# One-hots for 32 node pairs per VectorE operation in the count-matrix build, and a finer turn for the convolution beside it

## The chip, the cores and the metric

The program runs on one core of one Trainium2 chip. A core has a matrix engine (TensorE, PE in the profile, with its weight loads listed apart as PEld), a vector engine (VectorE, DVE), a scalar engine (ScalarE, ACT), GpSimd (POOL), a queue engine (SyncE, SP) and 16 DMA engines that they share. [...]The metric is the device time of one execution in microseconds (us). Before the change it is 3608.37 us, the median of three runs from 3608.08 to 3612.73.

## The reference, cut to what matters

Four graph layers follow one another on a graph of N = 6250 nodes, 64 features each, with 206250 directed edges given as `src` and `dst`, sorted by `dst`. Each layer is `x = x + f(relu(layernorm(x)))`. Three of the four `f` are sums over neighbours with degree weights; the first, where the change lies, is

```python
norm = dinv[s] * dinv[d]
msgs = norm[:, None] * x[s]
agg = segment_sum(msgs, d, num_segments=n)
return agg @ W.T + b          # twice: 64 -> 128, relu, 128 -> 64
```

The third layer runs a small network over every edge and sums its messages per node, and the fourth repeats the neighbour sum three times.

## The kernel before, in words

The nodes are padded to 49 blocks of 128 (NP = 6272). The kernel doesn't gather along the edges: it builds the dense matrix of edge counts once, as 8-bit floats, and every neighbour sum is then a product with it. Everything here lies in the function `fast`.

**The stages.** First each edge becomes a pair of numbers (destination with the high part of the source; the low part of the source), written to DRAM. GpSimd's indirect DMAs fetch, for each of GC = 25 chunks of 128 node pairs, the edges of the chunk: `near2` (L872) finds the exact start, and `run` (L881) fetches 128 edges for each pair. VectorE and ScalarE turn a run into two digits (L885, L887), TensorE transposes them (L890), and VectorE copies them into the table `key` (L891). The comparisons `less` (L900) with the products of L904 count the degrees. When the last chunk is in, `deg` and `by_col` (L913 to L920) go through DRAM (L921, L924) and give `deg_dst` (L927), the norms (L682 to L688), and the scaled features split into three bf16 parts, `U3` (L934, and `split`, L711 to L715).

**The build.** The matrix is made in CS = 14 strips of CW = 448 destination columns, 224 node pairs. `build(s, q)` makes GB = 16 pairs: VectorE compares `key` with a count and writes two one-hot tensors, `hd` (128 x 1568, bf16) and `lo` (128 x 2048, bf16), both by L852; then, for each of two PSUM tiles of SG = 8 pairs, TensorE does eight products `lo` x `hd` into `p_a` (L861), one for each pair, and ScalarE copies the tile into the strip as 8-bit floats (L865). NQ = 14 builds make a strip. `lo` and `hd` come from a pool with two buffers each, so the one-hots of a build can only be written once TensorE is done with those two builds earlier. The finished strip is written to DRAM on SP's queue (L997).

**The convolution beside it.** While strip s is built, strip s - 1 is multiplied with `U3`: 147 products (49 blocks x 3 parts, L748, with a few more for the loops, L949) accumulate in `p_sum`. `convolve` is a Python generator that gives its turn away after each fourteenth of the blocks; the loop over q calls one build and then one turn of the convolution. Strip 0 is built before the norms are known, inside the loop over chunks (from chunk 3 on, one build per chunk); in strip 1 the turns are held back until half of the strip and then doubled. Beside every second strip runs `hidden`, which turns two strips' sums into the next features: products L739, L731, L970 and L975 on TensorE, `z` (L962, L979) and the split (L713, L715) on VectorE, and copies on ScalarE.

**The order of the work.** In this stage no order is written out by hand: the framework's scheduler decides in which order each engine gets its instructions when the program is built. After it, the first neighbour product over the whole matrix (L1026) reads `piece` tiles from DRAM; its first load stands on SP's queue behind the write of the last strip. From there on TensorE's and VectorE's orders are written out by hand. The third layer starts near 1040 us and is paced by GpSimd's gathers (L1354); the fourth ends the kernel.

Of the kernel before, what the change touches and what calls it, by code (L numbers as in the profile page):

```python
# [8 lines left out]
F32 = mybir.dt.float32  # L9
# [7 lines left out]
P = 128  # L17
N = 6250
D = 64
NB = 49  # L20
# [567 lines left out]
SW = 128  # L588
NG = NP // 2
GC = -(-NG // P)  # L590
GB = 16
GQ = 2
CW = 448
CS = NP // CW
# [22 lines left out]
def fast(ctx, tc, bad, x, src, dst, edge_attr, W3, b3, W4, b4, w1, b1, w2, b2, Bw, Bb, Cw, Cb,  # L617
# [73 lines left out]
    def normed(h, X_c):  # L691

        m = stat.tile([P, CB], F32, name="m")
        nc.vector.tensor_reduce(m, X_c, axis=AX.X, op=OP.add)
        nc.vector.tensor_scalar_mul(m, m, 1.0 / D)
        nc.vector.tensor_sub(h, X_c, over_features(m))
        q = stat.tile([P, CB, D], F32, name="q")
        nc.vector.tensor_mul(q, h, h)
        v = stat.tile([P, CB], F32, name="v")
        nc.vector.tensor_reduce(v, q, axis=AX.X, op=OP.add)  # L700
        nc.scalar.activation(v, v, AF.Sqrt, bias=eps, scale=1.0 / D)
        nc.vector.reciprocal(v, v)
        nc.vector.scalar_tensor_tensor(h, h, 0.0, over_features(v), op0=OP.max, op1=OP.mult)

    def of_nodes(pool):

        return pool.tile([P, NB, 3, D], BF16, name="U3")
# [47 lines left out]
    early_pool = early.enter_context(tc.tile_pool(name="early_pool", bufs=1, reuse_waits="tile"))  # L755
    with ExitStack() as ph:

        ipool = ph.enter_context(tc.tile_pool(name="ipool", bufs=1, reuse_waits="tile"))
# [71 lines left out]
        with ExitStack() as ps:  # L830
            psum = ps.enter_context(tc.tile_pool(name="ps0", bufs=1, space=PSUM, reuse_waits="tile"))
            p = psum.tile([P, SG, P], F32, name="p_a", bufs=2)
            nc.tensor.transpose(p[:D, 0, :], W3_sb, ident)
            nc.vector.tensor_copy(W3T, p[:D, 0, :])
            p = psum.tile([P, SG, P], F32, name="p_a", bufs=2)
            nc.tensor.transpose(p[:, 0, :D], W4_sb, ident[:D, :D])
            nc.vector.tensor_copy(W4T, p[:, 0, :D])

            H0 = ipool.tile([P, NB, D], F32, name="H0")
            for c in range(NC):  # L840
                normed(H0[:, blocks(c), :], X[:, blocks(c), :])

            NQ = CW // 2 // GB
            strips = {0: spool.tile([P, NB, CW], COUNT, name="strip")}

            def build(s, q):

                at = (s * CW // 2) + q * GB
                lo = opool.tile([P, GB // GQ, 128, GQ], BF16, name="lo")
                hd = opool.tile([P, GB // GQ, 2 * NB, GQ], BF16, name="hd")  # L850
                for t, of, k in ((hd, turns, 0), (lo, count, 1)):
                    nc.vector.tensor_tensor(  # L852
                        t, of.unsqueeze(1).to_broadcast(t.shape),
                        key[:, k, at:at + GB].rearrange("p (h j) -> p h j", j=GQ)
                        .unsqueeze(2).to_broadcast(t.shape),
                        op=OP.is_equal)
                for r in range(GB // SG):
                    p = psum.tile([P, SG, P], F32, name="p_a", bufs=2)
                    for j in range(SG):
                        g = r * SG + j  # L860
                        nc.tensor.matmul(p[:, j, :2 * NB], lo[:, g // GQ, :, g % GQ],  # L861
                                         hd[:, g // GQ, :, g % GQ], start=True, stop=True)
                    col = 2 * (q * GB + r * SG)

                    nc.scalar.activation(  # L865
                        strips[s][:, :, col:col + 2 * SG].rearrange("p b (j l) -> p b j l", l=2),
                        p[:, :, :2 * NB].rearrange("p j (b l) -> p b j l", l=2), AF.Copy,
                        saturate=False)

            for c in range(GC):  # L870
                near2 = rpool.tile([P, LOOK, 2], F32, name="near2")
# [7 lines left out]
            for c in range(GC):  # L879
                run = rpool.tile([P, P, 2], F32, name="run")  # L880
                nc.gpsimd.indirect_dma_start(  # L881
                    out=run.rearrange("p e t -> p (e t)"), out_offset=None, in_=pairs[:, :],
                    in_offset=bass.IndirectOffsetOnAxis(ap=exact_i[:, c:c + 1], axis=0))
                digits = rpool.tile([P, 2, P], BF16, name="digits")
                nc.vector.tensor_scalar(digits[:, 0, :], run[:, :, 0], start_of[:, c:c + 1], None,  # L885
                                        op0=OP.subtract)
                nc.scalar.activation(digits[:, 1, :], run[:, :, 1], AF.Copy)  # L887
                p = psum.tile([P, 1024], BF16, name="p_dig")
                for k in range(2):
                    nc.tensor.transpose(p[:, k * P:(k + 1) * P], digits[:, k, :], ident_b)  # L890
                nc.vector.tensor_copy(key[:, :, c * P:(c + 1) * P],  # L891
                                      p[:, :2 * P].rearrange("p (k s) -> p k s", k=2))
                if 0 <= c - 3 < NQ:
                    build(0, c - 3)
                if c % 9 == 8 or c == GC - 1:
                    c0 = c // 9 * 9
                    p = psum.tile([P, 512], F32, name="p_node")
                    for k in range(3):
                        less = rpool.tile([P, 9 * P], BF16, name="less", bufs=2)
                        nc.vector.tensor_scalar(  # L900
                            less[:, :(c + 1 - c0) * P], key[:, 0, c0 * P:(c + 1) * P],
                            float(k * NB), None, op0=OP.is_lt)
                        for i in range(c0, c + 1):
                            nc.tensor.matmul(p[:, k * 9 + i - c0:k * 9 + i - c0 + 1],  # L904
                                             less[:, (i - c0) * P:(i - c0 + 1) * P],
                                             count[:, 1, 0:1], start=True, stop=True)
                    nc.vector.tensor_copy(
                        below[:, :, c0:c + 1],
                        p[:, :27].rearrange("p (k i) -> p k i", k=3)[:, :, :c + 1 - c0])
# [7 lines left out]
            p = psum.tile([P, 512], F32, name="p_node")  # L917
# [7 lines left out]
            p = psum.tile([P, 512], F32, name="p_node")  # L925
# [6 lines left out]
            for c in range(NC):  # L932
                u = wpool.tile([P, CB, D], F32, name="z", bufs=2)
                nc.vector.tensor_mul(u, H0[:, blocks(c), :], over_features(norm0[:, blocks(c)]))  # L934
                split(u, U3, c)
# [4 lines left out]
            def convolve(s, strip):  # L940

                p = psum.tile([P, 512], F32, name="p_sum", bufs=2)
                for q in range(NQ):
                    for b in range(q * NB // NQ, (q + 1) * NB // NQ):
                        if b == NB - 1:
                            for d in range(s * CW // P, -(-(s + 1) * CW // P)):
                                lo_, hi_ = max(d * P, s * CW), min((d + 1) * P, (s + 1) * CW)
                                for k in range(3):
                                    nc.tensor.matmul(  # L949
                                        p[k % 2 * D:(k % 2 + 1) * D, lo_ - s * CW:hi_ - s * CW],  # L950
                                        U3[:, d, k, :], ident_b[:, lo_ - d * P:hi_ - d * P],
                                        start=False, stop=False)
                        spread(p, U3, b, strip[:, b, :], CW)
                    yield
                if s % 2 == 0:
                    y[s // 2] = (wpool if s < CS - 2 else early_pool).tile([P, W], F32, name="y")
                nc.scalar.activation(y[s // 2][:, s % 2 * CW:(s % 2 + 1) * CW], p[:, :CW], AF.Copy)
# [25 lines left out]
            for s in range(CS):  # L983
                if s:
                    strips[s] = spool.tile([P, NB, CW], COUNT, name="strip")
                strip = strips[s]
                for q in range(NQ):
                    if s:
                        build(s, q)
                    if s == 1 and q < NQ // 2:  # L990
                        continue
                    for steps in beside * (2 if s == 1 else 1):
                        next(steps, None)
                for steps in beside:
                    for _ in steps:
                        pass
                nc.sync.dma_start(strip_of(s, slice(0, NB)), strip)  # L997
                beside = [convolve(s, strip)]
                if s and s % 2 == 0:
                    beside.append(hidden(s // 2 - 1, wpool, psum))  # L1000
# [496 lines left out]
    with ExitStack() as ph:  # L1497
# [5 lines left out]
        for layer in range(3):  # L1503
# [25 lines left out]
            else:  # L1529
                for s in range(CS):  # L1530
# [3 lines left out]
                    t = whole[:, :, s % 2 * CW:(s % 2 + 1) * CW]  # L1534
                    p = psum.tile([P, 512], F32, name="p_sum", bufs=2)
# [48 lines left out]
```

## Time and profile before

| what | value |
|---|---|
| device time, median of three runs | 3608.37 us |
| device time of the profiled execution | 3611.97 us |
| span of the profiled execution | 3610.2 us |
| busy over the span: TensorE, weight loads, VectorE, ScalarE, GpSimd | 84%, 59%, 54%, 34%, 46% |
| busy from 210 to 558 us: TensorE, weight loads, VectorE, ScalarE | 346.80, 229.57, 323.02, 255.43 of 348 us |
| mean TensorE clock, 100 to 157 us and 210 to 558 us | 0.57 and 1.00 |
| L852 `hd`, `lo`: operations, mean | 196 and 196; 974 and 1222 ns |
| L861 products, L865 copies | 3136; 392 at 820 ns |
| first product of the first convolution | 156.89 us |
| last one-hots begin, last strip's write is issued | 555.68 us, 559.11 us |

The profile is of one execution. Busy shares are means over stages with different limits, so the table also gives the stretch in which the matrix is built beside the convolution. [...]where one group follows another without a gap, the start times say more than the busy share. An operation's duration is from its start to its end as recorded; on VectorE the next one can start before that end, and the start-to-start time is what an operation costs in a full queue. "Idle before" names what released an engine.

### The profile page before, as it was taken

The page shows a single profiled execution, that of the slowest core. Times are in us where ns is not written, and L with a number is a line of the kernel's source. Part 1 is how long each engine was busy: PE and PEld are TensorE (multiplying, and loading weights), DVE is VectorE, ACT ScalarE, POOL GpSimd, SP SyncE. Part 2 cuts the span into 40 slices and gives each one's busy share as a digit, 9 for nine tenths or more (in the row PEclk, how much of TensorE's full clock was granted, in tenths as well). Part 3 has the DMA queues.
Part 4 walks back from the last instruction along what each step waited for, and adds up shares of the span by engine and source line. Part 5 has one row for each costly group of instructions (what it writes and reads, how often), then busy time and mean ns, then how long its engine had stood idle before and what let it go on. Part 6 is the DMA issues. An engine that isn't in the chain of part 4 may idle for free.

```text
span 3610.2 us, 59581 instructions
## 1 busy us (share of the span) xinstructions
PE 3039.4 (84%) x24393; PEld 2141.2 (59%) x24393; DVE 1954.2 (54%) x3899; ACT 1239.3 (34%) x2024; POOL 1665.0 (46%) x1889
## 2 busy tenths in 40 slices
PE   1699999999977777878878887878887888799999
PEld 0466667999954444444444444444454444489998
DVE  6899993532235546556555655655655565531111
ACT  1577772000023434434333443434433444210000
POOL 4200001000037777777777777777777777400000
PEclk9699999999988888889889888888988888799999
DMA  3233335565532223223323232322332322256664
GB/s 107 64 91 95 95 95 189 188 205 183 178 101 80 77 53 84 71 70 97 86 68 97 70 85 79 88 68 76 91 88 70 94 70 68 81 166 194 196 206 143
DMA packets 229312, 388.76 MB, mean 108 GB/s; under 512 B 137573, under 2 KB 139743, under 8 KB 228771
## 3 DMA queue, kind: packets, MB, share of 16 engines
q1 hardware_dynamic: 170420, 321.51, 28.3%
q0 software_dynamic: 55104, 60.65, 8.3%
q8 instruction: 193, 3.16, 0.4%
q10 hardware_dynamic: 3504, 2.70, 0.3%
q14 instruction: 91, 0.75, 0.1%
HBM read 340.47 MB, written 44.24 MB: 107 GB/s over the span
## 4 chain that ended last, share of the span: by engine, by line
POOL 35%; PE 35%; issue 14%; DMA 9%; DVE 5%; ACT 1%; POOLq 0%; DVEq 0%; SPq 0%; ACTq 0%
POOL v L1354 35%; PE p_acc L1026 21%; PE p_sum L748 7%; DMA v<-Vp_dram,src_g 7%; PE p_a L861 4%; DMA near<-pairs,begin_i 1%; PE p_node L739 1%; DMA piece<-A 1%; DVE lo L852 0%; DMA run<-pairs,exact_i 0%; PE p_acc L1023 0%; PE p_node L970 0%; PE p_bc L1380 0%; DMA X<-in_x 0%; PE p_node L975 0%
## 5 line engine op out<-in xcount | busy, mean ns | idle before, releaser
L1354 POOL DMA_INDIRECT v<-Vp_dram,src_g x1616 | 1592.1, 985 | 859.9 <-issue 828.6
L1026 PE MATMUL p_acc<-U,piece 128*128 128x192 bf16 x9604 | 817.7, 246 | 5.0 <-DMA piece<-A 5.0
L1026 PEld LDWEIGHTS <-piece 128*128 128x128 fp8e4 x9604 | 798.9, 98 | 17.0 <-DMA piece<-A 5.2
L1380 PE MATMUL p_bc<-BC,h 128*128 128x256 f32 x1616 | 585.8, 496 | 0.0
L1389 DVE TENSOR_TENSOR m<-gate,v 128x512 f32<-128x512 f32 x202 | 140.3, 694 | 762.5 <-DMA v<-Vp_dram,src_g 627.7
L1380 PEld LDWEIGHTS p_bc<-BC,h 128*128 128x128 f32 x1616 | 341.2, 234 | 154.7 <-issue 116.2
L1396 ACT ACTIVATE m<-m 128x512 bf16<-128x512 f32 x202 | 127.2, 630 | 821.9 <-DVE m L1391 821.9
L748 PEld LDWEIGHTS <-U 128*64 128x64 bf16 x4116 | 231.1, 112 | 215.4 <-issue 68.3
L1036 DVE TENSOR_REDUCE zg<-p_acc 128x128 f32<-128x384 f32 x112 | 56.3, 507 | 537.4 <-PE p_acc L1026 536.9
L865 ACT ACTIVATE strip<-p_a 128x784 fp8e4<-128x784 f32 x392 | 302.3, 820 | 112.6 <-PE p_a L861 112.0
L1376 PE MATMUL p_bc<-BC_b,ones 3*128 3x512 bf16 x404 | 180.9, 448 | 167.3 <-DVE m L1390 167.2
L1260 PE MATMUL p_sum<-ident_b,piece 128*128 128x128 bf16 x1372 | 154.9, 238 | 183.7 <-DVE junk L1266 183.4
L1260 PEld LDWEIGHTS <-piece 128*128 128x128 fp8e4 x1372 | 117.7, 107 | 318.8 <-issue 301.2
L1376 PEld LDWEIGHTS <-ones 3*128 3x128 bf16 x404 | 37.5, 93 | 439.4 <-DVE m L1390 235.3
L1366 PE MATMUL p<-h,w_d 128*128 128x512 f32 x404 | 253.5, 713 | 38.6 <-ACT h L1370 38.6
L748 PE MATMUL p_sum<-piece,U 128*64 128x448 fp8e4 x2058 | 238.1, 374 | 27.0 <-DVE junk L1266 18.7
L1370 ACT ACTIVATE h<-p,b_c 128x512 f32<-128x512 f32 x404 | 255.8, 684 | 12.9 <-PE p L1366 12.6
L1266 DVE SCALAR_TENSOR_TENSOR junk<-p_sum,there 128x512 bf16<-128x512 f32 (+1 forms) x392 | 242.1, 618 | 27.3 <-PE p_sum L1260 18.7
L748 PE MATMUL p_sum<-strip,U 128*64 128x448 fp8e4 x2058 | 242.0, 359 | 2.5 <-ACT U L711 1.4
L852 DVE TENSOR_TENSOR lo<-count,key 128x2048 bf16<-128x2048 bf16 x196 | 239.6, 1222 | 0.0
L861 PEld LDWEIGHTS <-lo 128*128 128x128 bf16 x3136 | 164.7, 103 | 98.6 <-DVE lo L852 75.8
L861 PE MATMUL p_a<-hd,lo 128*128 128x98 bf16 x3136 | 195.1, 217 | 32.6 <-DVE lo L852 31.1
(198 smaller groups left out, 3308.5 us busy)
## 6 DMA issues: line engine op xcount, KB each, us to landing
piece<-A SPq DMA_DIRECT2D x249, 784.0 KB, 4.3
e<-in_edge_attr SPq DMA_DIRECT2D x202, 256.0 KB, 2.7
A<-strip SPq DMA_DIRECT2D x14, 2744.0 KB, 13.1
v<-Vp_dram,src_g POOLq DMA_INDIRECT x1616
there<-A SPq DMA_DIRECT2D x28, 784.0 KB
pairs<-pair SPq DMA_DIRECT2D x1, 1616.0 KB, 5.3
Vp_dram<-v SPq DMA_DIRECT2D x7, 224.0 KB
out<-X SPq DMA_DIRECT2D x6, 224.0 KB
```

What stands on the lines that cost most here:

```text
L748: nc.tensor.matmul(p[half * D:(half + 1) * D, :w], U3[:, b, k, :], at_block, start=(i < 2), stop=(i >= 3 * n - 2))
L852: nc.vector.tensor_tensor(t, of.unsqueeze(1).to_broadcast(t.shape), key[:, k, at:at + GB].rearrange("p (h j) -> p h j", j=GQ) .unsqueeze(2 ...
L861: nc.tensor.matmul(p[:, j, :2 * NB], lo[:, g // GQ, :, g % GQ], hd[:, g // GQ, :, g % GQ], start=True, stop=True)
L865: nc.scalar.activation(strips[s][:, :, col:col + 2 * SG].rearrange("p b (j l) -> p b j l", l=2), p[:, :, :2 * NB].rearrange("p j (b l) -> ...
L1026: nc.tensor.matmul(p[d // 2][:, d % 2 * 3 * D:(d % 2 + 1) * 3 * D], t[:, b, d * P:(d + 1) * P], U3[:, k * CB + b, :, :].rearrange("p t f - ...
L1260: nc.tensor.matmul(p[:, a - a0, :], held["here", i, k][:, a, b * P:(b + 1) * P], ident_b, start=True, stop=True)
L1266: nc.vector.scalar_tensor_tensor(junk[:, :(a1 - a0) * P], p[:, :a1 - a0, :].rearrange("p a q -> p (a q)"), 15.5, of_there, op0=OP.min, op1 ...
L1354: nc.gpsimd.indirect_dma_start(out=v[:, j, :], out_offset=None, in_=Vp_dram[:, :], in_offset=bass.IndirectOffsetOnAxis(ap=src_g[:, g, j:j ...
L1366: nc.tensor.matmul(of[g][p], w, of[g].pop(x), start=True, stop=True)
L1370: nc.scalar.activation(of[g][t], of[g].pop(p), **how)
L1376: nc.tensor.matmul(p_bc[:, 4 * b:4 * b + 4].rearrange("p j o f -> p (j o f)"), ones, BC_b, start=True, stop=False)
L1380: nc.tensor.matmul(p_bc[:, 2 * q:2 * q + 2].rearrange("p j o f -> p (j o f)"), h2[:, q * P:(q + 1) * P], BC, start=False, stop=(k == 1))
```

## The change

GB goes from 16 to 32. A build covers 32 node pairs: one `hd` of 128 x 3136 and one `lo` of 128 x 4096, then four PSUM tiles. NQ, the builds per strip, becomes 7. `build` becomes a generator that gives its turn away after every second PSUM tile, the loop takes 2 x NQ steps, and the convolution is cut into 2 x NQ turns, so that a turn still follows on every 16 pairs. Strip 0's builds come at chunks 3, 5, ... 15 instead of at every chunk from 3 to 16. The one-hots' four buffers take twice the space; to make room, `H0`, the normed features, lies in the memory of `V3` instead of in a tile of its own (`V3` is first written much later, by `hidden`).

```diff
-GB = 16
+GB = 32
@@
-            H0 = ipool.tile([P, NB, D], F32, name="H0")
+            H0 = of_nodes(early_pool).rearrange("p b t f -> p (b t f)").bitcast(F32)[
+                :, :NB * D].rearrange("p (b f) -> p b f", f=D)
@@ build: at the end of the loop over PSUM tiles
+                    if r % 2:
+                        yield
@@ loop over chunks
-                if 0 <= c - 3 < NQ:
-                    build(0, c - 3)
+                if c >= 3 and c % 2 and (c - 3) // 2 < NQ:
+                    for _ in build(0, (c - 3) // 2):
+                        pass
@@ convolve
-                for q in range(NQ):
-                    for b in range(q * NB // NQ, (q + 1) * NB // NQ):
+                for q in range(2 * NQ):
+                    for b in range(q * NB // (2 * NQ), (q + 1) * NB // (2 * NQ)):
@@ loop over strips
-                for q in range(NQ):
+                for q in range(2 * NQ):
                     if s:
-                        build(s, q)
-                    if s == 1 and q < NQ // 2:
+                        if q % 2 == 0:
+                            built = build(s, q // 2)
+                        next(built, None)
+                    if s == 1 and q < NQ:
                         continue
                     for steps in beside * (2 if s == 1 else 1):
                         next(steps, None)
```

## The prediction

> **What bounds the kernel now.** I read the page first, to place the change: the build and the first convolution lie between 55 and 560 us, and the rest is another matter (from 1040 us GpSimd's gathers, then a full TensorE). Nothing after 560 us is touched by the diff, so the question is when that stage ends. I then took busy time by stretches. Columns: stretch, its length, then PE, PEld, DVE, ACT, POOL with counts, PE clock, DMA share, GB/s.
>
> ```profile
> 100.00:157.00 57.00, 33.20 (x370) 27.14 (x370) 47.60 (x88) 31.65 (x53) 12.18 (x12) 0.57 0.29 79
> 210.00:558.00 348.00, 346.80 (x4401) 229.57 (x4401) 323.02 (x330) 255.43 (x351) 0.00 (x0) 1.00 0.33 89
> ```
>
> Two regimes. From 210 us TensorE and VectorE both look full; before 157 us VectorE is the busiest and TensorE waits. [...]here the weight loads are at 66%; so I took start times from the chain that ended last (start, length, what), where the two are closest to a tie:
>
> ```profile
> 307.75 0.86 PE p_a L861 x16
> 308.62 1.26 PE p_sum L748 x12
> 309.87 0.86 PE p_a L861 x16
> 310.73 1.06 PE p_sum L748 x9
> 311.79 0.85 PE p_a L861 x16
> ```
>
> Each group starts when the one before ends. TensorE needs 0.855 + 1.06 and 0.855 + 1.26, so 4.03 us per 32 pairs, and leaves no gap. VectorE's timeline over the same time:
>
> ```profile
> 308.22 1.23 DVE L852 TENSOR_TENSOR lo<-count,key 128x2048 bf16<-128x2048 bf16 x1
> 309.36 0.98 DVE L852 TENSOR_TENSOR hd<-turns,key 128x1568 bf16<-128x1568 bf16 x1
> 310.24 1.23 DVE L852 TENSOR_TENSOR lo<-count,key 128x2048 bf16<-128x2048 bf16 x1
> ```
>
> Start to start: lo 1.135, hd 0.885, so 2.02 per 16 pairs and 4.04 per 32: a dead tie. What breaks it is `hidden`. Two strips repeat every 63.4 us (L739 starts at 209.65, 272.96, 336.34, 399.75). TensorE's share of that: 28 x 0.855 + 14 x (1.06 + 1.26) + hidden's 1.71 + 1.09 + 1.89 + 1.71 + L949's 0.7 = 63.5 us. VectorE's: 28 x 2.02 + 4 x 0.55 = 58.8. So TensorE is the bound, and VectorE waits for it; the waits of 209.65 to 526.49 us (who, for whom: total, times, longest) agree:
>
> ```profile
> PEld L861 <- DVE lo L852: 35.2, 95, 0.5
> DVE hd L852 <- PE p_a L861: 13.9, 15, 1.1
> ```
>
> The first line looks like the opposite, but its 0.37 us each is the weight queue's pause at a change of group, which also stands there with "issue" as the cause, while the matmuls of the chain run on without a gap.
>
> Before 157 us, the chain passes through VectorE and the loads of the edges:
>
> ```profile
> 119.78 0.70 ACT strip L865
> 120.50 0.83 ACT strip L865
> 121.45 6.60 DMA run<-pairs,exact_i
> 128.15 0.32 ACT digits L887
> 128.47 0.69 issue
> 129.17 5.60 DMA run<-pairs,exact_i
> 135.18 0.88 DVE hd L852
> ```
>
> Loads of `run` that took 2.67 us at 57.05 take 6 us here: strip 0's write went out at 121.34.
>
> [...]from durations, (1222 - 974)/(2048 - 1568) = 0.517 ns per element and 164 ns fixed; start to start, 0.521 ns and 68 ns. [...]lo takes 1222. [...]at 0.57, 16 products of L861 take 1.49 us, at 1.00 0.855.
>
> **The change part by part.**
>
> *One-hots.* 392 operations become 196. Estimated from the slope: hd 164 + 3136 x 0.517 = 1785 ns, lo 2282 ns; start to start 1.70 and 2.20, 3.90 us per 32 pairs against 4.04. VectorE gains 2 x 0.068 = 0.137 us per build of 32: 13.4 us over 98. From 167 us on, TensorE's own 63.5 us per two strips hide this: worth nothing there. Were TensorE not the cover it would be worth 0.96 us a strip.
>
> *TensorE's groups.* In the changed program as built, the steady order is the old one (16 products of p_a, then 9 or 12 of p_sum), with one group more per two strips (8 and 8 with 3 between). A change of group costs roughly 0.15 us (12 products of L748 take 1.26 in company, 12 x 0.0937 = 1.12 in the run of 147 at 558.75): 6 x 0.15 = +0.9. A few groups of p_a at 0.88 to 0.93 wait for lo, 0.17 us per two strips; gone: -1.0. Sum zero, ends -3 and +3.
>
> *Buffers.* Two of 32 pairs: hd of build n + 2 waits for all 32 products of n. VectorE has 3.90 for TensorE's 4.03; queued behind a waiting hd are lo and hidden's z, r and U. In the new queue z (L962) stands before a build that TensorE needs some 9.5 us after L739; z and that build take 0.6 + 3.9. At r and U, lo is done about 0.5 us ahead of need. Taken as zero; the end is a rival below.
>
> *H0's place.* V3's first write, near 224 us, is long after H0's last read (L934, near 165). The waits of `piece` loads and of GpSimd's DMAs are as before, but for two loads that lose a wait for VectorE. Nothing.
>
> *The start.* Here the order does change. VectorE's queue, up to by_col (L920), held 19 builds of 16; now 12.5 of 32, i.e. 25. Up to deg_dst 23 become 28, and before the first convolution starts TensorE has done 480 pairs' products instead of 384. Step by step, from 99.04 us (last `near` in):
>
> - VectorE then has 8 x 3.90 + 1.70 for builds 5 to 13's hd, plus 40 small operations, about 8.1: 41.0 us, by_col at 140.0 if never idle. Before, the same stretch was 33.5 of work and 10.4 idle (6.8 on late runs, the rest mostly on transposes queued behind p_a), by_col at 143.01. The larger builds sit in those gaps. Strip 0 is done some 5 us earlier, so its write meets runs 20 to 24 rather than 21 to 24, and three buffers of `run` hold the fetch back as before: I allow 3.5 idle, by_col 143.5. Ends: 140 (no idle), 147 (a lo of 2.2 us holds up the near gathers, a microsecond at each of four).
> - by_col to deg_dst took 8.4 (through DRAM, by two SP issues; VectorE has 6.1 of builds beside): 151.9.
> - deg_dst to the convolution's stream took 7.74 (to 159.16); hd, lo and hd between grow by 0.82 + 1.07 + 0.82: 10.4, so 162.3.
> - Then 168 products at 0.0937 and L949, 16.2, and 1.8 for the low clock at the start (before: 67 in 8.31): 180.3. The kernel before reached the same sum of work (480 pairs, 168 products) at 179.07 + 2 x 0.855 + 1.06 + 1.26 = 183.1.
>
> So 2.8 us less. The idle TensorE waits longer at the start, but has more of its work behind it. All that follows is TensorE-bound to the last p_a, then the fixed chain copy, strip write, first `piece` (559.72 + 19.2). Sum: -2.8 from the start, 0 in the steady part. The profiled execution took 3611.97 (span 3610.2) and would take 3609.2; the median 3608.4 becomes **3605.6 us**.
>
> **Rivals.**
>
> *A smooth start.* If the builds fill the idle time, by_col comes at 140 and the gain is 6: 3602. For it: 10 us of idle in VectorE's queue. Against: [...]a build stands where it stands.
>
> *A late start.* `near` and `run` wait behind operations of 2.2 us and three buffers: by_col 147 to 149, 3609 to 3611. For it: POOL's 1.25 us cadence leaves little slack. Against: POOL's own issues pace it until 97 us.
>
> *VectorE was the bound.* Then 0.137 x 7 x 13 = 12.5 us come off: 3596. For it: 94% busy. Against: the chain without gaps, and 13.9 us of waiting for TensorE.
>
> *Slower: two buffers starve TensorE at r and U.* Those wait for ScalarE's copies, which can stand behind two evictions (2 x 0.77 = 1.54 us); beyond the 0.5 us of slack that is 1.0 us each, 2.0 per two strips, 12 over six: 3605.6 + 12 = 3617. It decides once r or U comes more than 0.5 us late.
>
> **How the numbers follow.** Chances: forecast 0.58 (own range 3603 to 3608.5, from the ends of the sum), smooth start 0.15, late start 0.15, VectorE bound 0.05, starved 0.07. The measurement tells 0.2%, 7.2 us, from nothing. Faster by more: VectorE bound and a third of the smooth start, 0.10; slower: starved, 0.07; the rest, 0.83, is within. The range 3600 to 3611.5 takes in forecast, late start and most of the smooth one.
>
> **What would show it.** Right: L852's forms at about 1.78 and 2.28 us; PE without gaps from about 165 us and two strips every 63.4; the first convolution's product near 160, later than 156.89; the last strip's write about 3 us earlier than 559.11. Wrong: gaps of PE before L861 with VectorE as releaser, a two-strip period off by over 0.5 us, or by_col outside 140 to 147.

## The result and the profile after

The changed kernel takes 3618.78 us (median of 7 runs, 3615.66 to 3623.62) against 3610.11 for the kernel before (7 runs, 3606.16 to 3612.73): ratio 1.0031, 95% interval 1.0022 to 1.0040. It is slower by 8.7 us where 2.8 us less was forecast, and lies above the top of the range. The profiled execution took 3618.26 us (span 3616.5).

Busy time by stretches of the changed kernel (columns as before):

```profile
100.00:157.00 57.00, 30.99 (x361) 27.11 (x362) 46.07 (x70) 28.95 (x47) 22.34 (x16) 1.00 0.32 88
210.00:558.00 348.00, 347.25 (x4369) 229.35 (x4369) 312.72 (x176) 254.46 (x350) 0.00 (x0) 1.00 0.33 91
```

In the steady stretch VectorE's busy time fell by 10 us (323.02 to 312.72), and TensorE stayed full: worth nothing, as predicted. The number to look at is in the first line. GpSimd has 16 instructions where it had 12, and they take 22.34 us instead of 12.18. (The clock of 1.00 in that line, against 0.57 before, isn't a difference in speed: 16 products of L862 take 1.49 to 1.53 us there, as they mostly do in the kernel before, and 0.85 in the steady stretch. The trace of the changed kernel has no record of the clock before 177.7 us, and the view counts that as full.)

Milestones in the two traces, in us:

| | before | after | difference |
|---|---|---|---|
| last reduce of `near` ends | 99.12 | 107.51 | +8.4 |
| `by_col` starts | 143.01 | 157.15 | +14.1 |
| 480 pairs and 168 products of the convolution done | 183.17 | 192.09 | +8.9 |
| first `to_nodes` of the hidden chain (L739) | 209.65 | 218.58 | +8.9 |
| mean period of two strips after it | 63.37 | 63.82 | +0.45 |
| first `piece` load | 559.72 | 571.17 | +11.5 |

So there are two losses: about 9 us before 210 us, and 0.45 us in each later pair of strips. (The runs of the changed kernel alone differ by 8 us, 3615.66 to 3623.62, and in the undisturbed traces the part behind the first `piece` load takes 3045 to 3052 us, so one pair of traces doesn't give the 8.7 exactly.)

The smaller loss first. The chain that ended last, changed kernel, steady part:

```profile
235.75 1.06 PE p_sum L748 x9
236.81 0.48 PE p_a L862 x8
237.29 0.50 PE p_sum L748 x3
237.79 0.48 PE p_a L862 x8
238.27 1.06 PE p_sum L748 x9
```

This is the split group of the prediction, 8 and 8 products of `p_a` with 3 of `p_sum` between them. From 236.81 to 239.33 TensorE needs 2.52 us for 16 products of `p_a` and 12 of `p_sum`; unsplit they took 0.855 + 1.26 = 2.115. That is 0.40 us for two more changes of group, nearly the whole 0.45.

The larger loss shows on GpSimd. The timeline of the changed kernel, VectorE and then GpSimd (start, length):

```profile
71.41 1.78 DVE L853 TENSOR_TENSOR hd<-turns,key 128x3136 bf16<-128x3136 bf16 x1
73.86 2.29 DVE L853 TENSOR_TENSOR lo<-count,key 128x4096 bf16<-128x4096 bf16 x1
```

```profile
70.86 0.95 POOL L875 DMA_INDIRECT near<-pairs,begin_i  x1 [0.30 <-issue]
72.11 1.90 POOL L875 DMA_INDIRECT near<-pairs,begin_i  x1 [0.30 <-issue]
74.32 2.64 POOL L884 DMA_INDIRECT run<-pairs,exact_i  x1 [0.30 <-issue]
```

The gather at 72.11 starts inside `hd` (71.41 to 73.19) and ends 0.82 us after it, at 74.01. The one at 74.32 starts inside `lo` (73.86 to 76.15) and ends at 76.96, 0.81 us after it. The one at 70.86, which had run for 0.55 us when `hd` began, keeps its 0.95 us. None of them waits for a semaphore: the time is inside the instruction. The kernel before has the same, at half the length; again VectorE, then GpSimd:

```profile
66.89 1.22 DVE L852 TENSOR_TENSOR lo<-count,key 128x2048 bf16<-128x2048 bf16 x1
```

```profile
67.49 1.43 POOL L872 DMA_INDIRECT near<-pairs,begin_i  x1 [0.30 <-issue]
```

67.49 + 1.43 = 68.92, which is 0.81 us after `lo`'s end at 68.11. Up to the last gather of `near` GpSimd goes from one gather straight to the next in both kernels (0.30 us between them), so the whole stretch can be added up. Before: 37 gathers, 36 steps of 1.25 us, and 2.3 us of holding make 47.3 (47.46 from the first start to the last). After: 38 gathers (one more `run` stands ahead of the last `near`), 37 steps and 9.6 us of holding make 55.9 (56.05). The 8.6 us between them are 7.3 of holding and one step of 1.25. Holding is here the time by which the gathers exceed 0.95 us each.

### The profile page after: what moved, and what is told of

It is laid out like the page before. It is cut to its first block, busy times and chain, and to the rows that moved or that the text cites. A ratio compares the mean times of both kernels' runs of the same rounds, so it can differ in the third digit from the quotient of the medians.

```text
span 3616.5 us, 59295 instructions
## 1 busy us (share of the span) xinstructions
PE 3046.1 (84%) x24393; PEld 2148.2 (59%) x24393; DVE 1945.4 (54%) x3703; ACT 1240.5 (34%) x2024; POOL 1676.5 (46%) x1889
## 4 chain that ended last, share of the span: by engine, by line
PE 35%; POOL 34%; issue 14%; DMA 9%; DVE 6%; ACT 2%; POOLq 0%; DVEq 0%; SPq 0%; ACTq 0%
POOL v L1360 34%; PE p_acc L1032 20%; PE p_sum L748 7%; DMA v<-Vp_dram,src_g 7%; PE p_a L862 4%; PE p_node L739 1%; PE p_bc L1386 1%; DMA run<-pairs,exact_i 1%; DMA piece<-A 1%; DVE lo L853 0%; DMA near<-pairs,begin_i 0%; PE p_acc L1029 0%; PE p_node L974 0%; DVE hd L853 0%; DVE q L698 0%
## 5 line engine op out<-in xcount | busy, mean ns | idle before, releaser
L862 PE MATMUL p_a<-hd,lo 128*128 128x98 bf16 x3136 | 203.1, 220 | 33.9 <-DVE lo L853 24.2
L862 PEld LDWEIGHTS <-lo 128*128 128x128 bf16 x3136 | 170.6, 104 | 98.9 <-issue 67.0
L853 DVE TENSOR_TENSOR lo<-count,key 128x4096 bf16<-128x4096 bf16 x98 | 223.8, 2284 | 0.0
```

The costliest lines, as they stand in the source:

```text
L853: nc.vector.tensor_tensor(t, of.unsqueeze(1).to_broadcast(t.shape), key[:, k, at:at + GB].rearrange("p (h j) -> p h j", j=GQ) .unsqueeze(2 ...
```

## The experiments

Theory L: the loss is made at the start, where VectorE's operations of twice the length hold GpSimd's gathers. Against it stood S (the loss lies in the steady part or in the buffers of 32), O (what counts is the block of a build in VectorE's queue and the order around it) and H (H0's place). Later the start itself was parted into N (the hold of `near` makes the loss) and R (the longer queue and the held `run` gathers after `near` make it). In all diffs `pairs_of(s)` is the number of pairs in a build of strip s, and `w` the number in one VectorE operation.

One thing has to be known to read the numbers. The runs were made in sets, each beside the kernel before on the same chip. Three of the sets fell on chips on which the kernel before itself takes 4125 to 4160 us with a spread of over 1%, so that their ratios tell nothing under 0.3%. There TensorE and ScalarE also paused in the start, with operands ready: TensorE for 2 to 6 us at a time in the first of these sets, ScalarE for 11.5 and 5.9 us in e5_again. These chips are called disturbed below. Most of what ran on them was run again on chips where the kernel before takes 3609.6 to 3610.1 us; the table at the end of this section holds only those and the changed kernel's own result.

**Which strips lose: 16 first, then 32 (e1), and the reverse (e2).**

```diff
-    return 32
+    return 16 if s < 2 else 32      # e1; e2: 32 if s < 2 else 16
```

> Builds of 16 pairs for strips 0 and 1, of 32 for strips 2 to 13; the rest as in the changed kernel (H0's place, a turn after every second PSUM tile). Theory L (the loss is made at the start: VectorE's operations of 1.8 and 2.3 us hold up GpSimd's gathers of near and run): the start is that of the kernel before, last near reduce 99, by_col 143, 480 pairs and 168 products near 183; only the steady part's +0.45 us per two strips is left, so +2.5 us against the kernel before, ratio 1.0007. Rival S (the loss is in the steady part, or in two buffers of 32): as slow as the changed kernel, ratio 1.0025 to 1.003.

> The other half: builds of 32 pairs for strips 0 and 1, of 16 for strips 2 to 13. Theory L: last near reduce at 106 to 108, by_col at 154 to 158, the common point of 480 pairs and 168 products near 191 to 192, then a period of 63.4 us per two strips; +7 to +9 us, ratio 1.002 to 1.0025. Rival S: ratio 1.000.

On a chip of the disturbed kind e1 had its last `near` at 105.7, `by_col` at 149.8 and L739 at 216.3; e2 107.8, 157.9 and 218.6. Ratios 1.0001 (0.9973 to 1.0029) and 1.0007 (0.9987 to 1.0026). e2's start was the changed kernel's; e1's was not that of the kernel before. Both were run again:

> Builds of 16 pairs for strips 0 and 1, of 32 for strips 2 to 13, once more, since the first chip's times spread over 1% and its TensorE paused. Theory L (the loss is made at the start, by the length of VectorE's operations): on a chip without the pauses last near reduce at 99, by_col at 143, the steady part +2.5 us; ratio 1.0007. Rival S (steady part): 1.0025 to 1.003. Rival H (H0's place): last near reduce at 105, by_col at 149, ratio 1.002.

> Builds of 32 pairs for strips 0 and 1, of 16 for strips 2 to 13, once more. Theory L: last near reduce at 107 to 108, by_col at 157 to 158 as on the first chip, a period of 63.4 us per two strips, ratio 1.0015 to 1.0025. Rival S: 1.000.

e1: last `near` 100.1, `by_col` 143.9, L739 at 210.4, period 63.88, ratio 1.0005 (0.9996 to 1.0013). e2: 107.4, 156.8, 217.4, period 63.40, ratio 1.0020 (1.0013 to 1.0028). The two halves of the change carry the two losses: up to the first `piece` load e1 loses 2.7 us and e2 7.1 against the kernel before on the same chip, together 9.7; the changed kernel, on another chip, lies 10.6 above it. S falls.

**H0's place alone (e4).**

```diff
-            H0 = ipool.tile([P, NB, D], F32, name="H0")
+            H0 = of_nodes(early_pool).rearrange("p b t f -> p (b t f)").bitcast(F32)[
+                :, :NB * D].rearrange("p (b f) -> p b f", f=D)
```

> The kernel before with one edit of the change alone: H0 lies in the tile that later holds V3. Theory L and rivals S and O: nothing, ratio 0.9995 to 1.0005. Rival H (the shared place makes V3's first writes or the loads of the third layer wait): up to +3 us, ratio 1.001.

Ratio 0.9986 (0.9966 to 1.0007), but last `near` at 105.1 and `by_col` at 149.2, on the disturbed chip. H0's place or the chip? The kernel before was therefore run unchanged beside e1 to e3:

> The kernel before, instruction for instruction, as one more run beside the others on their chip. In the first set of runs TensorE paused for 2 to 6 us several times between 63 and 104 us, with its operands ready, in the kernels whose first strips have operations of 16 pairs, and last near reduce fell at 105. Theory C (that is the chip): on a chip that pauses, this kernel too has its last near reduce at 104 to 106 and by_col at 148 to 150; on one that doesn't, 99 and 143. Rival H (it is H0's place, which those kernels share and this one lacks): 99 and 143 on any chip.

It landed on an undisturbed chip: last `near` 99.6, `by_col` 143.6, L739 at 210.5, ratio 0.9999 (0.9991 to 1.0008). That doesn't tell what it would do on the other. What decides is e1_again on this same chip: it has H0's new place and starts within 0.5 us of it. H0's place costs nothing, and the 6 us of e4 go with the chip.

**Builds of 32 with two operations of 16 (e3).**

```diff
-                w = n
+                w = 16
```

> Builds of 32 pairs in buffers of 32, as in the changed kernel, but each one-hot is made by two VectorE operations of 16 pairs. Theory L (the length of one operation counts): no GpSimd gather takes over 1.45 us, the sums of 25 near and 25 run fall back to 25 to 26 us each, last near reduce at 99 to 101, by_col at 143 to 147; ratio 0.9995 to 1.001. Rival O (what counts is that a build of 32 stands in VectorE's queue as one block, at every second chunk, whatever its operations): last near reduce at 104 to 108, by_col over 150, ratio 1.002 to 1.003.

> Builds of 32 pairs, each one-hot made by two VectorE operations of 16 pairs, once more. Theory L: the sums of 25 near and 25 run fall to 25 to 27 us each; last near reduce at 99 to 101, by_col at 143 to 147, ratio 0.9995 to 1.001. Rival O (the block of a build in VectorE's queue counts, whatever its operations): by_col over 150, ratio 1.002 to 1.003.

First try, on the disturbed chip: last `near` 101.8, `by_col` 149.8, ratio 0.9997 (0.9971 to 1.0024). Second: 98.9, 145.3, L739 at 210.4, period 63.41, ratio 1.0002 (0.9994 to 1.0010). The gathers of the changed kernel and of e3 (busy us and mean ns, then the idle time before them):

```profile
L884 POOL DMA_INDIRECT run<-pairs,exact_i x25 | 34.6, 1384 | 19.6 <-DVE digits L888 7.7 <-ACT strip L866 5.2 <-issue 5.0
L875 POOL DMA_INDIRECT near<-pairs,begin_i x25 | 29.2, 1169 | 50.9 <-DVE begin L807 43.6 <-issue 6.7 <-DVE key L894 0.3
```

```profile
L902 POOL DMA_INDIRECT run<-pairs,exact_i x25 | 29.6, 1185 | 20.8 <-ACT digits L908 7.0 <-ACT strip L877 4.8 <-DVE digits L906 3.5
L893 POOL DMA_INDIRECT near<-pairs,begin_i x25 | 25.7, 1029 | 50.8 <-DVE begin L815 43.5 <-issue 5.8 <-DMA near<-pairs,begin_i 0.9
```

With the large builds and buffers kept, splitting the operation gives back the whole start, and the steady part too: no `p_a` group is split there (the scheduler makes that split only where the steady strips have the single long operation). `near` falls to 25.7 as expected; `run` stays at 29.6, over the 25 to 27 expected: the gathers at 104.48 and 109.92, for instance, start 0.4 us into a `lo` of 1.22 us and take 1.63 us each. Single gathers also reach 1.47 us (`near`) and 2.00 us (`run`), where no more than 1.45 was expected. As the order changed with the split, O isn't yet excluded for `by_col`.

**Is it the bf16 rate or the length? (e6).** The constants that the keys of strip 0's first 112 pairs are compared with become float32:

```diff
+                    wide = s == 0 and at < 7 * GB
-                    for t, of, k in ((hd, turns, 0), (lo, count, 1)):
+                    for t, of, k in ((hd, turns_f if wide else turns, 0),
+                                     (lo, count_f if wide else count, 1)):
```

> A look at the hold itself. Builds of 16 pairs, but for the first 112 pairs of strip 0 the two constant rows of digits that the one-hots are compared with are float32 copies, so that an operation of 16 pairs takes about as long as one of 32 in bfloat16 (estimate: twice the 0.517 ns per element, hd about 1.8 us, lo about 2.3). Theory L1 [...]: near and run that start inside one end 0.82 us after it, up to 2.6 us each. Theory L2 (only an operation at the doubled bfloat16 rate holds it): they keep 0.94 to 1.0 us beside the float32 ones, and stretch to 1.4 beside the later bfloat16 ones. The time is not the point; slower by 0 to 8 us.

4138.72 us, one run on a disturbed chip, which says nothing of the time. VectorE's forms (mean ns last but one) are of the length aimed at:

```profile
L871 DVE TENSOR_TENSOR lo<-count_f,key 128x2048 bf16<-128x2048 f32 x7 | 16.0, 2287 | 0.0
L871 DVE TENSOR_TENSOR lo<-count,key 128x2048 bf16<-128x2048 bf16 x9 | 11.0, 1218 | 0.0
```

and the timeline has, VectorE and then GpSimd:

```profile
62.34 2.29 DVE L871 TENSOR_TENSOR lo<-count_f,key 128x2048 bf16<-128x2048 f32 x1
```

```profile
61.91 0.95 POOL L900 DMA_INDIRECT near<-pairs,begin_i  x1 [0.30 <-issue]
63.17 2.28 POOL L909 DMA_INDIRECT run<-pairs,exact_i  x1 [0.30 <-issue]
```

63.17 + 2.28 = 65.45, 0.82 after `lo`. The gathers are held to 29.3 and 33.6 us in sum, like the changed kernel's (29.2 and 34.6), by builds of 16 pairs at half the rate: from `hd` and `lo` 1.04 ns per element with the float32 constants (1787 and 2287 ns) and 0.52 with both in bf16 (970 and 1218). The gather ends as L1 expected, and L2 falls: beside these one-hots the length of the operation counts, not its rate and not the number of pairs.

**The smaller dose (e5): builds of 8 pairs for strips 0 and 1.**

```diff
-    return 16
+    return 8 if s < 2 else 16
```

> The dose on the other side: strips 0 and 1 by builds of 8 pairs (operations of about 0.57 and 0.70 us by the slope), the rest of 16. Theory L: no gather over 1.2 us, the 50 gathers at 48 to 49 us in sum, last near reduce at 97 to 98; by_col at 141 to 144; against it VectorE pays its fixed 0.137 us per build more often, 2 to 4 us in the stretch, mostly in its idle time. Ratio 0.999 to 1.0005. Rival (the gathers don't set the start): by_col at 146 to 148, 1.0005 to 1.001.

> Strips 0 and 1 by builds of 8 pairs, the rest of 16, once more. On the chip of the first try no gather was held over 1.23 us, but pauses of that chip put last near reduce at 106. Theory L, on a chip without pauses: last near reduce at 97 to 98, by_col at 140 to 143; first `to_nodes` at 208 to 210; ratio 0.999 to 1.000. Rival (below operations of 16 pairs the hold no longer sets the start): last near reduce at 99, first `to_nodes` at 210 to 213, ratio 1.000 to 1.001.

Both runs fell on disturbed chips. Of the dose they show what was expected: no gather above 1.23 us, `near` at 24.4 and 24.5, `run` at 25.8 and 25.7. Up to the last `near` the holding is 0.9 us in e5_again, with operations of 8 pairs; it is 2.3 to 3.7 with 16 (before, b0_again, e1_again, e3_again) and 9.6 to 9.9 with 32 (changed, e2_again, e9_again). Of the time they show nothing: ratios 0.9998 (0.9962 to 1.0033) and 0.9991 (0.9964 to 1.0017), last `near` at 105.9 and 105.4, and in the second ScalarE stood still twice (from 63.5 to 75.0 and for 5.9 us before 94.4). Whether 8 pairs would make a better start stays open.

**Two attempts on the start (e7, i1), both on a disturbed chip.** e7 is the changed kernel with strip 0's builds begun later (what is left of the strip is built after the loop over chunks):

```diff
-                elif step == 2 and c >= 3 and c % 2 and (c - 3) // 2 < NQ // 2:
+                elif step == 2 and c >= 13 and c % 2:
```

> The changed kernel with one edit: strip 0's builds of 32 pairs begin ten chunks of edges later (at chunk 13 instead of 3), so that most of the long operations no longer lie beside the gathers of near. Theory L: the gathers of near keep their 0.95 us until the builds begin, last near reduce at 98 to 102; by_col at 147 to 152, since GpSimd's late runs still meet them; first piece load at 563 to 568 against 571 in the changed kernel, ratio 1.0005 to 1.0015. Rival O (VectorE's queue before by_col is simply longer): by_col at 155 or later whatever near does, ratio 1.0025 or more.

Both sides missed. The scheduler put four builds of 32 before the last `near` all the same: last `near` at 113.3, `by_col` at 150.5, L739 at 218.6, first `piece` load at 571.2, ratio 1.003 (1.0006 to 1.0054). It took no cause away, and decides nothing.

i1 is the kernel before with H0's new place and

```diff
-name="rpool", bufs=3
+name="rpool", bufs=5
```

> An attempt at a better start: the kernel before with H0 in V3's later tile, and five buffers instead of three for near, run and digits. The order as built then has all 25 gathers of near before the first one-hot, and the run gathers with one-hots after them. Theory L: near is never held, last near reduce at 80 to 83; runs are held by operations of 1 to 1.2 us only; by_col at 130 to 142, first piece load 1 to 8 us earlier; ratio 0.998 to 1.000. Rival (VectorE's work up to by_col bounds the start; the early near only moves idle time ahead): by_col at 143 to 146, ratio 1.000 to 1.001.

`near` is never held (23.8 us in sum) and ends at 89.0, later than the 80 to 83 expected, but `by_col` comes at 153.5 and L739 at 220.9; ratio 1.0043 (1.0014 to 1.0073). VectorE, with no one-hot to make before the gathers of `near` are through, has 14.5 us of work from 45 to 90 us against 24.8 in the kernel before, and has the rest still to do later. Here an early `near` alone was no gain.

**The four corners of the start (e8, e9).** e8 has short operations beside `near`, and then the changed kernel's order; e9 the reverse.

```diff
+                w = 16 if s == 0 and at0 < 128 else n                  # e8
+                w = 16 if s == 0 and at0 >= 128 or s == 1 else n       # e9
```

> The changed kernel, but the one-hots of strip 0's first 128 pairs (those beside the gathers of near) are made by two operations of 16 pairs each; from there on its order is the changed kernel's, 26 half builds of 32 before by_col, 480 pairs before the first convolution. Theory N (the hold of near makes the loss): last near reduce at 99 to 100, by_col at 148 to 151, first `to_nodes` near 210 to 212, period 63.83; +2 to +4 us against the kernel before, ratio 1.0005 to 1.001. Theory R (the late runs and the longer queue before by_col make it): first `to_nodes` at 216 to 219, +7 to +9 us, ratio 1.002 to 1.0025.

> The other corner: operations of 32 pairs for strip 0's first 128 pairs, of two times 16 for the rest of strips 0 and 1, of 32 again from strip 2 on. Theory N: last near reduce at 107, by_col at 152 to 155, first `to_nodes` at 216 to 219; +7 to +10 us, ratio 1.002 to 1.003. Theory R: last near reduce at 107, but first `to_nodes` at 211 to 213, since the queue after it is short; +1 to +4 us, ratio 1.0005 to 1.001.

> The changed kernel, instruction for instruction, once more beside the two corners: last near reduce at 107 to 108, by_col at 157, first `to_nodes` at 218.6, period 63.83, first piece load at 571; ratio 1.002 to 1.003.

All three on a disturbed chip: L739 at 220.0, 215.2 and 219.0 (last `near` 102.9, 107.9, 107.5; `by_col` 159.0, 150.3, 156.8), ratios 0.9991 (0.9971 to 1.0011), 1.0008 (0.9980 to 1.0035) and 1.0007 (0.9982 to 1.0031). The kernels with long operations beside `near` start there as elsewhere; e8, with its pauses, spoke for R. Run again:

> Short operations beside near, the changed kernel's order after it, once more. On a chip without pauses (kernel before: first `to_nodes` at 210.5; changed: 218.6): theory N (the hold of near makes the loss) 210 to 212, ratio 1.0005 to 1.001; theory R (the longer queue and the held runs after near make it) 216 to 219, ratio 1.002 to 1.0025. The last set, though disturbed, spoke for R: by_col 56 us after the last near reduce.

> Long operations beside near, two of 16 pairs after it up to the end of strip 1, once more. Theory N: last near reduce at 107, first `to_nodes` at 216 to 219, ratio 1.002 to 1.003. Theory R: last near reduce at 107, by_col at 148 to 151, first `to_nodes` at 211 to 215, ratio 1.001 to 1.002, of which 0.0006 is the period of 63.83 us in the steady part.

| kernel, operations beside `near` / after it | last `near` | `by_col` | L739 | period | first `piece` | ratio |
|---|---|---|---|---|---|---|
| before, 16 / 16 | 99.6 | 143.6 | 210.5 | 63.36 | 560.6 | 0.9999 |
| e1, 16 / 16, then 32 | 100.1 | 143.9 | 210.4 | 63.88 | 563.3 | 1.0005 |
| e2, 32 / 32, then 16 | 107.4 | 156.8 | 217.4 | 63.40 | 567.6 | 1.0020 |
| e3, 16 / 16 in builds of 32 | 98.9 | 145.3 | 210.4 | 63.41 | 560.5 | 1.0002 |
| e8, 16 / 32 | 98.4 | 151.8 | 211.5 | 63.82 | 564.1 | 1.0013 (1.0007 to 1.0019) |
| e9, 32 / 16 | 107.7 | 150.4 | 214.9 | 63.82 | 567.5 | 1.0019 (1.0010 to 1.0028) |
| changed, 32 / 32 | 107.5 | 157.2 | 218.6 | 63.82 | 571.2 | 1.0031 (1.0022 to 1.0040) |

Read L739. Long operations beside `near` cost 4.5 us with a short rest (214.9 against 210.4) and 7.1 with a long one (218.6 against 211.5). The long rest costs 1.1 us behind a punctual `near`, hardly more than the 0.9 by which two executions of the kernel before differ here (209.65 and 210.5), and 3.7 behind a late one. Neither theory holds alone: e8 came out as N expected, e9 as R did. What lies beside `near` is the larger part, and R adds to it where `near` is already late. The corners also differ in more than the hold: with long operations beside `near` the scheduler puts 38 gathers up to the last `near`, with short ones in builds of 32 only 36, and two steps are 2.5 of the 9 us by which the last `near` is late. No run keeps that order and takes the hold away. e8 also shows that `by_col` is a poor measure here: it is 6.5 us later than in e3, but TensorE has 480 pairs behind it at the first convolution instead of 368, and all but 1.1 us comes back. No kernel of these beats the kernel before.

## Why the prediction was wrong

**What bounds, and the one-hots' worth: right.** `hd` takes 1.78 and `lo` 2.28 us as estimated, and VectorE's saving changes nothing while TensorE is full. The waits of 218.58 to 537.69 us of the changed kernel (in total, times, longest):

```profile
PEld L862 <- issue: 46.8, 125, 0.8
...
DVE hd L853 <- PE p_a L862: 12.3, 10, 2.2
```

The weight queue's pauses at a change of group now stand almost all with "issue"; 2.7 us in the five periods stand against `hd`, and the matmuls run on. The rival of the two buffers forecast a slower kernel (3617), but e3 has builds of 32 in the same buffers and a period of 63.41 us; the kernel is slower for another reason.

**The start: the step that failed.** The prediction said "from 99.04 us (last `near` in)", and went on from there as if the change could not move that time. It did, by 8.4 us. It had noted that "POOL's own issues pace it until 97 us", and took the length of these issues for GpSimd's own. It is VectorE's as well. The view of the tile `near` of the kernel before had it (duration in ns: least, median, most):

```profile
L872 POOL DMA_INDIRECT near<-pairs,begin_i x25: 942/946/1432, 48.1 to 95.6; - x25
```

The three long ones (1.35 to 1.43 us) all start inside a one-hot; the very first gather (1.12 us) doesn't. The prediction took the median and left the maximum unread.

Then the steps to `by_col`, 143.5 forecast and 157.15 measured: `near` is 8.4 later, VectorE's work 41.85 us instead of 41.0, and its idle time 7.8 instead of 3.5. (For the same stretch of the kernel before the prediction read 33.5 of work and 10.4 idle; its trace has 34.8 and 9.1.) The idle time has late `run` transfers behind it, in the chain that ended last of the changed kernel:

```profile
112.82 4.90 DMA run<-pairs,exact_i
...
125.84 8.04 DMA run<-pairs,exact_i
...
135.01 6.23 DMA run<-pairs,exact_i
```

Each of these times contains a held gather (to 114.80 at the first) or strip 0's write, which went out at 126.45, or both. "The larger builds sit in those gaps" was argued from sums; the order in the queue left 7.8 us of gaps. How much of these the held gathers make, and how much the write, isn't shown.

The steps after `by_col` were roughly right: to `deg_dst` 6.4 (forecast 8.4), on to the stream 9.7 (10.4), to the common point 18.8 (18.0). So the common point came at 192.1 instead of 180.3.

**The late start** was the right rival with too small an end: it allowed for "a microsecond at each of four", by way of waits in the queue and of three buffers. Eight gathers were held ahead of the last `near`, inside the instruction, with 7.3 us more in sum than before, and 147 to 149 became 157.

**TensorE's groups: mis-sized.** "6 x 0.15 = +0.9" and "gone: -1.0" for a sum of zero. A split, which is two more changes of group and not one, costs 0.40 us, and the small waits for `lo` that were to go are worth nothing in the period: 63.41 in e3, where the split is absent, 63.37 before. Measured: 0.45 per two strips, 2.7 us in e1.

**H0's place: right**, by e1_again.

**What stood in the trace.** With the maximum of that row and the timelines of VectorE and GpSimd side by side (67.49 + 1.43, 0.81 us after `lo`), the loss could have been priced: up to 50 gathers, of which each one that starts inside a one-hot ends no earlier than 0.82 us after it. The runs show the hold and its length; by what means a one-hot holds a gather, they don't show.

## What to carry to other kernels

Before a VectorE operation is made longer to save its fixed cost (0.068 us start to start here, an estimate from `hd` and `lo` of the kernel before), look at what GpSimd issues beside it: here an indirect gather that starts inside a one-hot ends 0.82 us after it, so that the length of one operation, and not only the sum of all, sets the pace of the gathers (38 of them with 9.6 us of holding in the changed kernel, 37 with 2.3 before). Read the maximum of a group as well as its median; where a few in a row of equal instructions are long, look for a cause outside them. And where a saving is hidden in one stage, look for what the same edit costs in the others: here 10 us of saved VectorE time were worth nothing, and a start of 150 us lost 9.

## What the runs showed of the hardware

- A GpSimd gather (0.95 us alone) that starts inside a one-hot of VectorE ends 0.81 to 0.83 us after the one-hot's end, or at its own 0.95 if that is later. In the traces of the two kernels, with operations of 0.97 and 1.22 us before and 1.78 and 2.29 after, 23 of the 24 gathers in which it can be seen did so; the other, at 125.84 in the changed kernel, ended 0.94 us after it (a `less` begins 0.4 us behind the one-hot), as one at 94.34 in e2_again did 0.92 after, with a `less` behind it too. The gather at 63.17 in e6 does the same beside a float32 form of 2.29 us (0.82). One that starts before the one-hot isn't held, even if by 0.06 us only (100.75 and 100.81 in the changed kernel, 0.95 us long).
- Two tensor operands aren't needed for it. Two gathers that started inside a `less` (one bf16 tensor against a number, 0.45 us) ended 0.81 us after it: that at 95.45 us in e1_again took 1.05 us, that at 121.45 in the kernel before 1.23. Six that started inside the reduce of `near` (`junk`, 0.32 us) weren't held (73.20, 89.07 and 94.32 in the kernel before, 95.08 in b0_again, 98.55 in e3_again, 98.19 in e8_again), nor were four inside the copy from PSUM into `key` (0.27 to 0.29 us; 69.23 and 90.32 before, 129.63 changed, 69.16 in e3_again): each took 0.95 us and ended 0.65 to 0.78 us after the operation.
- A bf16 comparison whose constant operand is float32 takes 2287 ns for 2048 elements in e6, against 1218 with both in bf16.
- Two more changes between groups of matmuls with different operands cost TensorE 0.40 us in the steady stretch, where 16 products of `p_a` take 0.855 us (236.81 to 239.33 us in the changed kernel: 2.52 against 2.115).
- On some chips TensorE and ScalarE paused in the first 110 us, operands ready: TensorE for 2 to 6 us at a time between 63 and 104 us in the first set, ScalarE for 11.5 and 5.9 us in e5_again. By L739, kernels with short operations beside `near` were later there (e1 by 5.9 us, e8 by 8.5); those with long ones had pauses too (two of ScalarE's, 5.3 us in sum, in the changed kernel), but came within 1.2 us of the undisturbed time (e2 1.2, e9 0.3, changed 0.4). The cause wasn't found.
